# Two attention and expert layers on one core: an addition moved behind the maxima, a copy tied to order, and gathers one step sooner

## The chip, the cores and the metric

The kernel runs on one core of a Trainium2 chip. Its time is that of one launch in microseconds (us) on the device. The core's engines run beside each other, each through its own queue in order: TensorE does matmuls (in the profile PE, and PEld for its weight loads), VectorE (DVE), ScalarE (ACT) and GpSimd (POOL) do the rest, and SyncE (SP) issues most of the transfers (DMAs).

## What is computed

The reference, cut to what matters (4 batches of 512 tokens by 256; a context of 1601 rows per batch; all in float32):

```python
x = x + cross_attention_0(ctx, layernorm(x))   # 8 heads of 128, keys from context and latents, with projections
x = x + experts_0(layernorm(x))                # 8 experts, 2 per token, capacity 512 rows per expert, gelu (tanh)
x = x + cross_attention_1(ctx, layernorm(x))   # 8 heads of 32, queries from x, keys and values from the context
x = x + experts_1(layernorm(x))                # 8 experts, 2 per token, no capacity, gelu (exact), biases
```

In `cross_attention_1` the weights are a softmax over the 1601 context rows:

```python
attn = softmax(q @ k.T * 32 ** -0.5)           # per batch and head: 512 x 1601
out  = attn @ v
```

## The kernel before

The program is one long stream of steps with four stages: the first attention (128 steps of a batch, a head and 128 queries), the first expert layer, the second attention, and the second expert layer. Small work of one stage (routing, layernorms, gathers, projections) is hung by hand into the steps of another, in lists such as `later` and `at`.

**Second attention.** It runs in 16 units. A unit is (batch `b`, half `o` of the channels, half `f` of the queries): four heads of 32 channels, and 256 queries. Units 0 to 3 are batch 0, 4 to 7 batch 1, and so on. A unit has seven steps (`PER_UNIT`), each over 256 context rows; the last has 65. All engines but SyncE follow the program's order here, because the loop stands in `in_order(*computing)`.

One pass of the loop over `step` emits, in this order:

1. `weights(u, s)`: TensorE puts an offset (L1587, four matmuls, one per head) and the scores (L1597) of this step into four banks; ScalarE takes the exponential into the tiles `pT` (L1611; step 0 writes the tiles `sum`).
2. For the step before (`held`): `weigh` (L1633), weights times values, and `add_weights` (L1623).
3. In step 2 of a unit, `closing` of the unit before: transposes and small matmuls (L1671, L1672), then DVE's `inv` and `got` (L1680, L1682), and a closing sum into `x` on GpSimd (L1689).
4. `maxima` (L1329, L1340): TensorE makes a piece of the next unit's scores again in another layout, into four banks, and DVE takes the maxima `tops` out of them, one instruction per head. A unit has six pieces of 512 rows and one short piece of 2 x 65. The short piece falls into step 3.
5. `total` (L1652): matmuls with ones that sum the weights over the context rows.
6. The list `at[step]`: whatever was hung into this step.

`add_weights` adds the tiles `pT` of the steps 1, 3 and 5 onto those of step 0 (`ADDED = (1, 3, 5)`), so that `total` has fewer tiles to sum. Batch 3 adds only step 3 (`ADDED_LATE`). It acts on the `held` step: the tiles of step 1 are added in step 2, those of step 3 in step 4, those of step 5 in step 6. Each time it is two DVE instructions (L1623) of 128 x 1024.

The scores, the offsets and the small tiles beside them share one pool of seven banks:

```python
ps_s = st.enter_context(tc.tile_pool(name="c_ps_s", bufs=7, space=PSUM))
```

A step takes four banks for `weights` and four for `maxima`, and more where small work needs one, so a tile's bank is the one that was taken seven tiles before.

**Gathers for later batches.** `collect(b + 1)` gives eight steps: each fills a tile `g` with zeros (L361) and gathers the rows that the first expert layer made for 128 tokens (L362), both on GpSimd. `add_collected` then multiplies `g` by its share and adds it to `x` (L381, L382, on GpSimd, twice per 128 tokens). After that `queries(b + 1)` takes the layernorm statistics of `x` (L145, L146, L155 on DVE, a root on ScalarE, the rest of L176 to L179 on DVE, L183 on GpSimd) and projects it (L1289). `s0` is the first step of batch `b` (28 per batch); with `b` = 1 and 2, batches 2 and 3 are gathered at `s0 - 14` and the seven steps after it, and their sums follow in two steps.

**Second routing.** `route2(b - 1)` is a generator that is resumed at listed steps; its parts touched here are GpSimd's `extra`, `cnt`, `earlier` and `taken` (L533 to L541), TensorE's two matmuls with them (L547, L550), DVE's `counted` (L554), place arithmetic (L565 to L577), the transposes of its weights (L559) and the addition of a bias product to `x` (L627, which reads a bank of the same pool).

**First routing.** `choose` in `route` picks two experts per token, counts them per expert, and carries the counts of earlier tokens from tile to tile in `taken`: `earlier` (L318) keeps for each of four tiles what was taken before it, and L319 adds the tile's own counts. TensorE uses both (L324, L327). This runs for batches 0 to 2 within the first attention, and for batch 3 within the first expert layer. Outside the second attention the order on an engine is a scheduler's, within what the data allow, unless an instruction is given to `keep_in_program_order`.

Of the kernel before, what the change touches and what calls it, by code (L numbers as in the profile page):

```python
# [13 lines left out]
ALU = mybir.AluOpType  # L14
# [62 lines left out]
def rows_of(i, n, tail):  # L77
    return tail if i == n - 1 else P
# [6 lines left out]
def xattn_ffn_twice(ctx: ExitStack, tc: tile.TileContext, a: dict, out: bass.AP):  # L85
    nc = tc.nc
# [112 lines left out]
    def transposed(psum, tag, dst, src, n):  # L199
        for c in range(DC):  # L200
            turn_part(psum, tag, dst, src, n, c)
# [47 lines left out]
    taken = const.tile([P, E], F32, name="taken")  # L249
# [7 lines left out]
    def route(b, rt, wide_rt, psum, tag):  # L257
# [5 lines left out]
        def small(name):  # L263
            return rt.tile([P, NT], F32, tag=name, name=name)

        def wide(name):
            return rt.tile([P, NT, E], F32, tag=name, name=name)

        def spread(t):
            return t.unsqueeze(2).to_broadcast([P, NT, E])  # L270
# [6 lines left out]
        def choose():  # L277
            xnT = wide_rt.tile([P, DC, S], F32, tag="xnT", name="xnT")
            transposed(psum, tag, xnT, xn, NT)
            ps = psum.tile([P, NT, E], F32, tag=tag, name="ps_l")  # L280
            for t in range(NT):
                for c in range(DC):
                    nc.tensor.matmul(
                        ps[:, t, :],
                        lhsT=xnT[:, c, t * P : (t + 1) * P],
                        rhs=wr[:, c, :],
                        start=c == 0,
                        stop=c == DC - 1,
                    )
            sc, m = wide("sc"), small("m")  # L290
            nc.vector.tensor_copy(sc, ps)
            nc.vector.tensor_reduce(m, sc, AX.X, ALU.max)
            nc.vector.tensor_tensor(sc, sc, spread(m), ALU.subtract)
            nc.scalar.activation(sc, sc, AF.Exp)
            nc.vector.tensor_reduce(m, sc, AX.X, ALU.add)
            nc.vector.reciprocal(m, m)
            nc.vector.tensor_tensor(sc, sc, spread(m), ALU.mult)


            hot, chosen = [], []  # L300
            for k in range(2):
                pk, ck, hk, cand = prob[k][:, mine_b], small(f"c{k}"), wide(f"hot{k}"), wide("cand")
                nc.vector.tensor_reduce(pk, sc, AX.X, ALU.max)
                nc.vector.tensor_tensor(cand, sc, spread(pk), ALU.is_equal)
                nc.vector.scalar_tensor_tensor(cand, cand, -64.0, iota, ALU.mult, ALU.add)
                nc.vector.tensor_reduce(ck, cand, AX.X, ALU.min)
                nc.vector.tensor_tensor(hk, cand, spread(ck), ALU.is_equal)
                nc.vector.tensor_scalar(ck, ck, 64.0, None, ALU.add)
                if k == 0:
                    nc.vector.scalar_tensor_tensor(sc, hk, -4.0, sc, ALU.mult, ALU.add)  # L310
                hot.append(hk)
                chosen.append(ck)


            cnt, earlier = wide("cnt"), wide("earlier")
            nc.vector.tensor_tensor(cnt, hot[0], hot[1], ALU.add)
            for t in range(NT):
                nc.vector.tensor_copy(earlier[:, t, :], taken)  # L318
                nc.vector.tensor_tensor(taken, taken, cnt[:, t, :], ALU.add)  # L319
            if b in (0, B - 2, B - 1):  # L320
                nc.vector.tensor_copy(reached[:, (0, B - 2, B - 1).index(b), :], taken)
            ps = psum.tile([P, NT, E], F32, tag=tag, name="ps_c")
            flat = "p t e -> p (t e)"
            nc.tensor.matmul(  # L324
                ps.rearrange(flat), lhsT=before, rhs=cnt.rearrange(flat), start=True, stop=False
            )
            nc.tensor.matmul(  # L327
                ps.rearrange(flat), lhsT=ones, rhs=earlier.rearrange(flat), start=False, stop=True
            )
            for k in range(2):  # L330
                off, at, mine = small("off"), small("at"), wide("mine")
                nc.vector.tensor_tensor(mine, hot[k], ps, ALU.mult)
                nc.vector.tensor_reduce(off, mine, AX.X, ALU.add)
                nc.vector.scalar_tensor_tensor(at, chosen[k], float(CAP), off, ALU.mult, ALU.add)
                nc.vector.tensor_scalar(off, off, float(CAP), NOWHERE, ALU.is_ge, ALU.mult)
                nc.vector.tensor_tensor(at, at, off, ALU.add)
                nc.vector.tensor_copy(slot[k][:, mine_b], at)
# [305 lines left out]
    def fetched(e, half):  # L643
        n = 1 if half and e in FEW else CT
        sx = b_two.tile([P, CT, D], F32, tag="sx", name="sx")[:, :n]
        nc.sync.dma_start(sx, slots(slot_x, e, half, n))
        w1 = b_two.tile([P, DC, FF], F32, tag="w1", name="w1")
        w2 = b_two.tile([P, FC, D], F32, tag="w2", name="w2")
        nc.sync.dma_start(w1, a["w1"][e].rearrange("(c p) f -> p c f", p=P))
        nc.sync.dma_start(w2, a["w2"][e].rearrange("(c p) d -> p c d", p=P))  # L650
        return e, half, sx, w1, w2
# [34 lines left out]
    with ExitStack() as st:  # L686
# [410 lines left out]
        for n in range(n_steps + 4):  # L1097
            b, h, t = n // (H0 * NT), n // NT % H0, n % NT
# [278 lines left out]
    with ExitStack() as st:  # L1377
# [75 lines left out]
        first = fetched(0, 1)  # L1453
# [103 lines left out]
    with ExitStack() as st:  # L1557
# [18 lines left out]
        def keys_of(s):  # L1576
            return range(2 * s, min(2 * s + 2, NM))
# [39 lines left out]
        def added(u):  # L1617
            return ADDED if units[u][0] < B - 1 else ADDED_LATE

        def add_weights(u, s, pTs):  # L1620
            if s in added(u):
                for to, pT in zip(sums[u], pTs):
                    nc.vector.tensor_tensor(to, to, pT, ALU.add)  # L1623

        def weigh(u, s, pTs, ps):

# [15 lines left out]
        def total(u, s, pTs, ps):  # L1642

            of = [(s, pTs)] if s and s not in added(u) else []
            if s == PER_UNIT - 1:
                of.append((0, sums.pop(u)))
            for s0, tiles in of:
                js = keys_of(s0)
                r = rows_of(js[-1], NM, TAIL)
                for k in range(len(js)):  # L1650
                    for i in range(HG):
                        nc.tensor.matmul(  # L1652
                            ps[i * DH1 : (i + 1) * DH1, QH:],
                            lhsT=ones[:r, :DH1],
                            rhs=tiles[i // 2][:r, i % 2, k * QH : (k + 1) * QH],
                            start=False,
                            stop=s0 == 0 and k == 1,
                            skip_group_check=True,
                        )
# [120 lines left out]
        for b in range(B):  # L1780
            s0 = per_batch * b
            if b:
                place(s0, route2(b - 1, one, side, "s", far=far), routed if b + 1 < B else last_routed)
            if b + 1 < B:
                got, steps = collect(b + 1)
                first = s0 if b == 0 else s0 - 14
                for k, f in enumerate(steps):
                    put(first + (k // 2 if b == 0 else k), f)
                for t in range(NT):
                    put(  # L1790
                        (first + 4 if b == 0 else first + 7) + t // 2,
                        lambda b=b, got=got, t=t: add_collected(b + 1, got, (t,), nc.gpsimd),
                    )
                place(s0, queries(b + 1, qTs), asked[b + 1])
# [19 lines left out]
        held, ending = None, {}  # L1814
        for step in range(PER_UNIT * n_units + 5):
            u, s = divmod(step, PER_UNIT)
            fresh = (u, s, weights(u, s)) if u < n_units else None
            if held:
                if held[1] == 0:
                    ps_of = ps_o.tile([P, 2 * QH], F32, tag="o", name="ps_o1")  # L1820
                weigh(*held, ps_of)
                add_weights(*held)
            next(ending.pop(step, iter(())), None)
            for g in ahead.pop(step, ()):
                maxima(*g)
            if held:
                total(*held, ps_of)
                if held[1] == PER_UNIT - 1:
                    ending[step + 2] = closing(held[0], ps_of)
                    next(ending[step + 2])  # L1830
            for f in at.pop(step, []):
                f()
            held = fresh
# [6 lines left out]
    with ExitStack() as st:  # L1840
# [252 lines left out]
        more = [lambda e=e: first_tile(e) for e in range(2, E)]  # L2093
# [12 lines left out]
        for i in range(n):  # L2106
            w, xT, to, share = here
# [153 lines left out]
```

## Time and profile before

| what | value |
|---|---|
| time, median of 3 runs (lowest, highest) | 2684.9 us (2683.66, 2690.97) |
| the profiled execution | 2684.01 us |
| its span, first to last instruction | 2682.0 us |
| mean granted TensorE clock | 0.997 |
| busy share of TensorE, DVE, ACT, POOL | 98%, 49%, 33%, 14% |
| second attention, about 1861.9 to 2385 us | TensorE busy 507.6 of 523.1 us, DVE 377.2, ACT 261.2, POOL 193.5 |
| two additions L1623, start of the first to start of what follows | 2.27 us |
| one maximum L1340, 128 x 512 and 128 x 130 | 0.69 and 0.29 us, 0.6 and 0.2 us apart |
| one pair L381 and L382 on GpSimd | 1.72 us |

The profile is of one execution. Its timeline gives for each instruction the start from the beginning of the span, its length, the engine, the line, what it writes and reads, and in brackets how long the engine sat idle before it and what ended that. The view of waits sums such idle time by who waited for whom. A busy TensorE is not TensorE at its peak, because matmuls are pipelined and their ends are modelled.

### The profile page before, as it was taken

The numbers are of one execution on the slowest core, as the hardware profiler recorded it, in microseconds if no ns is written. First come the engines' busy times: TensorE is split into PE (matmuls) and PEld (weight loads), VectorE is DVE, ScalarE is ACT, GpSimd is POOL, SyncE is SP. The second block draws the span as 40 slices with busy tenths as digits, with TensorE's granted clock in tenths as the row PEclk, the third lists the DMA queues.
The fourth block names the chain that finished last, engine by engine and source line by source line (L and its number), as shares of the span: only waits on it lengthen the run. The fifth ranks groups of instructions, "written<-read, shape, count | busy, mean of one in ns | idle before, by whom it ended". The sixth has DMA issues, their size and how long they took to land. (4 is left out here: it accounts for less than half of the span.)

```text
span 2682.0 us, 38424 instructions
## 1 busy us (share of the span) xinstructions
PE 2625.5 (98%) x14748; PEld 1785.6 (67%) x14748; DVE 1319.7 (49%) x2307; ACT 898.2 (33%) x1589; POOL 372.2 (14%) x485
## 2 busy tenths in 40 slices
PE   7999999999999999999999999999999999999997
PEld 3666676666666666667667678877454454468887
DVE  6544547644456544454544442134777777642111
ACT  4333233323333322333233322122554445452221
POOL 0000000100000100000100000101442531334442
PEclk9999999999999999999999999999999999999999
DMA  6444434433443433433443464643443100036663
GB/s 181 120 114 113 101 93 114 104 93 89 107 115 87 115 94 87 98 91 86 108 99 89 124 200 142 209 158 101 126 126 120 64 32 5 23 113 187 193 219 78
DMA packets 191324, 302.91 MB, mean 113 GB/s; under 512 B 41783, under 2 KB 113272, under 8 KB 188440
## 3 DMA queue, kind: packets, MB, share of 16 engines
q1 hardware_dynamic: 152392, 218.33, 29.4%
q0 software_dynamic: 14160, 46.31, 5.9%
q10 hardware_dynamic: 24576, 35.68, 5.2%
q8 instruction: 119, 1.95, 0.3%
q14 instruction: 77, 0.63, 0.1%
HBM read 111.46 MB, written 51.07 MB: 61 GB/s over the span
## 5 line engine op out<-in xcount | busy, mean ns | idle before, releaser
L995 DVE TENSOR_REDUCE top<-ps_s 128x1 f32<-128x2113 f32 x128 | 301.7, 2357 | 592.1 <-PE ps_s L987 587.1
L1024 PE MATMUL ps_o<-pT,v 128*128 128x256 f32 x2176 | 519.1, 380 | 0.4 <-DVE inv L1002 0.4
L987 PE MATMUL ps_s<-kT,qT 128*128 128x512 f32 (+1 forms) x1280 | 486.6, 524 | 2.6 <-ACT attn L1001 2.6
L1024 PEld LDWEIGHTS ps_o<-pT,v 128*128 128x128 f32 x2176 | 407.9, 190 | 112.6 <-issue 66.8
L1001 ACT ACTIVATE attn<-ps_s,top 128x2113 f32<-128x2113 f32 x128 | 258.9, 2023 | 492.7 <-DVE top L995 461.6
L987 PEld LDWEIGHTS ps_s<-kT,qT 128*128 128x128 f32 x1280 | 241.1, 190 | 249.3 <-issue 237.9
L1016 DVE STREAM_TRANSPOSE pT<-swapped 128x2176 f32<-128x2176 f32 x128 | 312.4, 2441 | 34.0 <-DMA swapped<-attn 25.8
L1340 DVE TENSOR_REDUCE tops<-ps_s 128x1 f32<-128x512 f32 (+2 forms) x428 | 251.6, 649 | 140.8 <-PE ps_s L1329 140.7
L933 PE MATMUL ps_k<-kvin,wkv 128*128 128x512 f32 (+2 forms) x640 | 259.3, 528 | 2.8 <-DVE kvin L823 2.4
L970 PE MATMUL ps_v<-wkv,kvin 128*128 128x256 f32 x1088 | 254.5, 381 | 2.1 <-ACT v L977 2.1
L970 PEld LDWEIGHTS ps_v<-wkv,kvin 128*128 128x128 f32 x1088 | 204.5, 190 | 36.1 <-ACT v L977 6.2
L1611 ACT ACTIVATE pT<-ps_w 128x512 f32<-128x512 f32 (+1 forms) x384 | 184.3, 565 | 119.4 <-PE ps_w L1597 118.6
L949 ACT ACTIVATE kT<-ps_k,bqk 128x512 f32<-128x512 f32 (+1 forms) x192 | 101.0, 555 | 268.9 <-PE ps_k L933 126.0
L933 PEld LDWEIGHTS ps_k<-kvin,wkv 128*128 128x128 f32 x640 | 116.0, 192 | 75.4 <-issue 64.4
L977 ACT COPY v<-ps_v 128x512 f32<-128x512 f32 x144 | 80.0, 561 | 215.5 <-PE ps_v L970 131.0
L1329 PE MATMUL ps_s<-kv,qT 32*128 32x512 f32 (+1 forms) x1024 | 123.8, 550 | 0.0
L1597 PE MATMUL ps_w<-qT,kv 32*128 32x256 f32 (+1 forms) x1664 | 118.3, 382 | 0.0
L757 POOL TENSOR_TENSOR x<-x,bo 128x256 f32<-128x256 f32 x16 | 11.8, 768 | 724.1 <-DVE lat L183 532.1
L670 PE MATMUL ps_h<-sxT,w 128*128 128x256 f32 (+1 forms) x512 | 108.0, 367 | 0.6 <-DVE x L1045 0.6
L1393 PE MATMUL ps_y<-w,hT 128*128 128x256 f32 x480 | 107.8, 380 | 0.0
L670 PEld LDWEIGHTS ps_h<-sxT,w 128*128 128x128 f32 x512 | 91.9, 190 | 17.7 <-issue 4.2
L1393 PEld LDWEIGHTS ps_y<-w,hT 128*128 128x128 f32 x480 | 90.3, 190 | 14.9 <-issue 2.4
(328 smaller groups left out, 2736.2 us busy)
## 6 DMA issues: line engine op xcount, KB each, us to landing
swapped<-attn SPq DMA_DIRECT2D x1536, 68.0 KB
swapped<-attn ACTq DMA_DIRECT2D x512, 68.0 KB
w<-in_w_dram SPq DMA_DIRECT2D x32, 1024.0 KB
rows_b<-empty SPq DMA_DIRECT2D x36, 530.0 KB
w_e<-in_wall_dram SPq DMA_DIRECT2D x5, 2052.0 KB
cw<-in_ctxT_dram SPq DMA_DIRECT2D x4, 1601.0 KB
ctx_b<-in_ctx_dram SPq DMA_DIRECT2D x3, 1536.0 KB
slot_x<-scrap SPq DMA_DIRECT2D x8, 512.0 KB
```

The lines of the kernel that those rows point to most:

```text
L670: nc.tensor.matmul(ps[:, f, :], lhsT=w1[:, c, (f0 + f) * P : (f0 + f + 1) * P], rhs=sxT[:, c, :], start=c == 0, stop=c == DC - 1,)
L933: nc.tensor.matmul(ps[:, :n], lhsT=wkv[:, c, hs], rhs=kvin[:, c, : n // 32, k, :] if k < 4 else flat_kvin[c][:, left : left + P], start=c ...
L970: nc.tensor.matmul(ps[:, k, :], lhsT=flat_kvin[c][:, j * P : (j + 1) * P], rhs=wkv[:, c, cols], start=c == 0, stop=c == DC - 1,)
L987: nc.tensor.matmul(flat[:, j0 : j0 + n], lhsT=qT[:, t * P : (t + 1) * P], rhs=kT[:, j0 : j0 + n], start=True, stop=True,)
L995: nc.vector.tensor_reduce(top, flat[:, :L], AX.X, ALU.max, negate=True)
L1001: nc.scalar.activation(attn[:, :L], flat[:, :L], AF.Exp, bias=top, accum_out=total)
L1016: nc.vector.transpose(pT[:, :, k * P : (k + 1) * P].rearrange("p c (a i) -> p a c i", a=4), swapped.rearrange("p a (c i) -> p a c i", i=32),)
L1024: nc.tensor.matmul(ps, lhsT=v[:, j - parts[part][0], (h % 2) * DH0 : (h % 2 + 1) * DH0], rhs=pT[:, j, :], start=j == 0, stop=j == NB - 1,)
L1329: nc.tensor.matmul(pss[i][:, at : at + n], lhsT=qTs[b][rows, o, q0 : q0 + P], rhs=kvs[b][0][o][rows, j0 : j0 + n], start=True, stop=True,)
L1340: nc.vector.tensor_reduce(tops[u][:, t : t + at // n, some, j0 // 512], of, AX.X, ALU.max,)
L1393: nc.tensor.matmul(ps[:, t, :], lhsT=hT[:, f, t * P : (t + 1) * P], rhs=w2[:, f, :], start=f == 0, stop=f == FC - 1,)
L1611: nc.scalar.activation(pT[:r, i, :n], pss[2 * h + i][:r, :n], AF.Exp)
```

## The change

Four places are edited. In `choose`, the copy L318 of the first tile is kept in program order (for every batch). In `add_weights` a parameter `behind` is new; the loop calls it for step 1's tiles behind `maxima` and not before them. The gathers of batches 2 and 3, and with them their sums, are hung one step sooner (`s0 - 15`). `asked`, the steps at which the queries' layernorm is taken, is unchanged.

```diff
             for t in range(NT):
-                nc.vector.tensor_copy(earlier[:, t, :], taken)
+                carried = nc.vector.tensor_copy(earlier[:, t, :], taken)
+                if t == 0:
+                    tc.keep_in_program_order(carried)
                 nc.vector.tensor_tensor(taken, taken, cnt[:, t, :], ALU.add)
...
-        def add_weights(u, s, pTs):
+        def add_weights(u, s, pTs, behind=False):
             if s in added(u):
                 for to, pT in zip(sums[u], pTs):
-                    nc.vector.tensor_tensor(to, to, pT, ALU.add)
+                    more = nc.vector.tensor_tensor(to, to, pT, ALU.add)
+                    if behind:
+                        tc.keep_in_program_order(more)
...
                 got, steps = collect(b + 1)
-                first = s0 if b == 0 else s0 - 14
+                first = s0 if b == 0 else s0 - 15
                 for k, f in enumerate(steps):
                     put(first + (k // 2 if b == 0 else k), f)
...
                 weigh(*held, ps_of)
-                add_weights(*held)
+                if held[1] != 1:
+                    add_weights(*held)
             next(ending.pop(step, iter(())), None)
             for g in ahead.pop(step, ()):
                 maxima(*g)
             if held:
+                if held[1] == 1:
+                    add_weights(*held, behind=True)
                 total(*held, ps_of)
```

## The prediction

> **What bounds the kernel now.** First the page's busy line: TensorE (PE) is the bound, and the rest is idle time of 56 us, so a change of order can only act through what PE waits for.
>
> ```profile
> PE 2625.5 (98%) x14748; PEld 1785.6 (67%) x14748; DVE 1319.7 (49%) x2307; ACT 898.2 (33%) x1589; POOL 372.2 (14%) x485
> ```
>
> Then the waits of PE, who waited for whom (us in total, times, longest). The first line lies in the second attention (1861.9 to about 2385 us), the second at one place of the first attention.
>
> ```profile
> PE ps_w L1587 <- DVE tops L1340: 13.7, 30, 1.4
> ...
> PE ps_v L970 <- ACT v L977: 2.1, 1, 2.1
> ```
>
> Then the timeline of one step that the change touches: unit 6, steps 2 and 3 (I write 6.2, 6.3; a step begins where PE starts the four L1587). VectorE (DVE) first, then PE; columns are start, length, instruction, count, and in brackets the idle time before it with its releaser.
>
> ```profile
> 2074.47 2.35 DVE L1623 TENSOR_TENSOR sum<-sum,pT 128x1024 f32<-128x1024 f32 x2
> ...
> 2077.92 2.48 DVE L1340 TENSOR_REDUCE tops<-ps_s 128x1 f32<-128x512 f32 x4 [0.31 <-PE ps_s L1329]
> ...
> 2080.97 0.19 DVE L513 TENSOR_TENSOR wb<-wb,totw 128x32 f32<-128x32 f32 x1
> 2081.52 0.89 DVE L1340 TENSOR_REDUCE tops<-ps_s 128x2 f32<-128x130 f32 x4 [0.36 <-PE ps_s L1329]
> 2082.33 2.35 DVE L1623 TENSOR_TENSOR sum<-sum,pT 128x1024 f32<-128x1024 f32 x2
> ```
>
> ```profile
> 2077.72 0.39 PE L1587 MATMUL ps_w<-below,ones_b 6*128 6x512 bf16 x3
> 2078.66 0.37 PE L1587 MATMUL ps_w<-below,ones_b 6*128 6x512 bf16 x1 [0.55 <-DVE tops L1340]
> ...
> 2082.43 0.40 PE L1587 MATMUL ps_w<-below,ones_b 6*128 6x512 bf16 x4
> ```
>
> Seven banks rotate. With four for the weights and four for the maxima in a step, the fourth weights bank of a step is the one that the first maximum of the step before reads. So PE stops at 2078.66, when the first of the maxima that began at 2077.92 has ended. That costs 0.94 us (the fourth start less the first). But those maxima did not wait for the addition, done at 2076.82: the bracket names PE's own scores. The same 0.55 us gap with PE as the releaser stands in units 1, 2, 3, 4, 6 and 10.
>
> **The addition (12 units, batches 0 to 2).** Nothing is added or removed: two L1623 per unit move behind the four maxima of step 2. As built, the orders of PE, ScalarE and SP are the same before and after; only DVE's and POOL's differ. Two additions hold DVE's queue for 2.27 us (at 2093.36 and 2094.49, next start 2095.63). What was their cover, DVE waiting for PE's closing transposes, is left empty; behind them now stand the small work of step 2, the short maxima of step 3 (0.2 us apart) and the bank that step 4's fourth L1587 needs. In unit 6: DVE free at 2081.16, later by 2.27 = 2083.43 (scores ready 2081.52, so the queue decides); first short maximum and handing over 0.34, 2083.77; PE wants the bank at 2082.43. Stall 1.34. That such lateness stops PE the trace shows already, where layernorm statistics make 7.3's short maxima late (PE, PE, DVE):
>
> ```profile
> 2116.56 0.39 PE L1587 MATMUL ps_w<-below,ones_b 6*128 6x512 bf16 x3
> 2117.17 0.37 PE L1587 MATMUL ps_w<-below,ones_b 6*128 6x512 bf16 x1 [0.21 <-DVE tops L1340]
> ```
>
> ```profile
> 2116.85 0.86 DVE L1340 TENSOR_REDUCE tops<-ps_s 128x2 f32<-128x130 f32 x4
> ```
>
> The same sum for the others, as DVE free before / step 4 begins / stall: unit 1 1910.53 / 1911.48 / 1.66; 2 1942.90 / 1944.93 / 0.58; 3 1976.64 / 1977.58 / 1.67; 5 2044.53 / 2047.00 / 0.14; 9 2188.06 / 2190.54 / 0.13; 10 2224.38 / 2225.66 / 1.33; 11 2256.65 / 2258.16 / 1.10, less 0.08 because its step-2 maxima did start late. Unit 4 has 1.98 us of query projection between: none. Unit 0 is the one case that the edit is good for: maxima at 1873.43 could start at 1872.9, a gain of 0.53, and lose 0.60 in step 4. Unit 3 pays 0.25 more, since its root's input (L155) comes late to ScalarE ahead of step 5's exponentials. Unit 8: behind the additions stands L627 (2151.79 to 2152.47), which reads a bank that PE takes next for a quarter of step 3's scores (one more tile is in the rotation here); it would end 2.27 later, at 2154.74, and PE wants the bank at 2152.90: 1.9, rounded up. The later addition (step 3's) ends before step 4's scores in each unit, since PE is late too. Without unit 7: 1.66+0.58+1.67+0.25+0.14+1.34+1.9+0.13+1.33+1.02+0.07 = 10.1.
>
> The trace does not show the additions beside GpSimd (POOL) at the new places; beside its arithmetic two of them took 2.73 instead of 2.35 (2107.72), so each stalled unit lies between 0 and 0.4 more. I take 0: POOL is mostly idle there.
>
> [...]
>
> **Gathers and sums one step sooner.** POOL runs in order, so I look at what the sums overtake. The eight gathers themselves (1.0 each to issue, on POOL's own queue; their buffers are long free) only move into POOL's idle time. For batch 2 (units 1 to 3) they and the sums overtake a closing sum that nobody awaits: nothing. DVE's two additions there no longer meet POOL's arithmetic, which I count as nothing too. For batch 3 the built order puts the sums of two row tiles, four pairs L381 and L382, ahead of the carried counts L538 to L541. POOL, then PE:
>
> ```profile
> 2099.80 1.04 POOL L362 DMA_INDIRECT g<-slot_y,slot  x1 [0.27 <-POOL g L361]
> 2100.88 0.25 POOL L538 TENSOR_TENSOR cnt<-hot,hot 128x32 f32<-128x32 f32 x1
> ...
> 2102.68 0.19 POOL L540 COPY earlier<-taken 128x8 f32<-128x8 f32 x1
> ...
> 2106.51 0.92 POOL L381 TENSOR_SCALAR g<-g,prob 128x256 f32<-128x256 f32 x1
> 2107.51 0.72 POOL L382 TENSOR_TENSOR x<-x,g 128x256 f32<-128x256 f32 x1
> 2108.22 2.94 POOL L381 TENSOR_SCALAR g<-g,prob 128x256 f32<-128x256 f32 x1
> ```
>
> ```profile
> 2107.11 0.39 PE L550 MATMUL ps_c<-earlier,ones 128*128 128x32 f32 x2
> ```
>
> A pair takes 1.72 (2106.51 to 2108.22, rounded up), four 6.9. The last copy ends at 2102.87, so at 2109.77; L550 wants it at 2107.11. The slack of 4.2 is used up and PE waits 2.7, with the whole of step 7.2 queued behind it. In return:
>
> ```profile
> 2120.56 0.43 DVE L145 BATCH_NORM_STATS2 st<-x 128x6 f32<-128x256 f32 x1 [2.30 <-POOL x L382]
> ```
>
> DVE waits here for the last sum, and PE pays: steps 7.4 and 7.5 lose 0.61 and 2.36 on L1587 (2122.34 to 2124.70), and 0.87 on 7.5's scores (2.01 instead of 1.14), held by exponentials behind a late root; 3.84 in all. After: DVE free at 2113.84 + 2.27 additions + 1.21 place work (unit 11's row) + 1.07 statistics = 2118.39, first maximum 2118.73, PE at 2116.56: 2.17; step 7.5 has no bank stall, but the root is still late, 0.85. So 3.02 for 3.84, a gain of 0.8; unit 7 nets 2.7 - 0.8 = +1.9.
>
> On L381's 2.94: it lies beside the two additions, its equals take 0.92. [...]
>
> **Counts tied to order.** Four copies of 0.17 come 0.2 us into their own chain; PE's L327 follows it, 0 to 0.2 each; I take 0, four matmuls of L1035 lie beside it. One evacuation (L124) goes ahead of a 0.17 us copy (L321): nothing. But the copy for the last batch leaves this place (DVE, PE):
>
> ```profile
> 1315.56 0.17 DVE L318 COPY earlier<-taken 128x8 f32<-128x8 f32 x1 [7.52 <-DMA slot_x<-xn,slot]
> 1315.66 2.36 DVE L995 TENSOR_REDUCE top<-ps_s 128x1 f32<-128x2113 f32 x1
> ```
>
> ```profile
> 1323.58 0.70 PE L970 MATMUL ps_v<-wkv,kvin 128*128 128x256 f32 x2 [2.07 <-ACT v L977]
> ```
>
> It held DVE for a scatter whose buffer it takes over; the maximum behind it started 2.8 late (scores done 1312.83), the exponential and ACT's v copies after it too, and PE lost 2.07. All of it comes back: 2.07, bounded by 0 and 2.8.
>
> **Sum.** 10.1 + 1.9 - 2.1 = +9.9, all on PE, so it moves the end. The profiled execution took 2684.01 (span 2682.0 and 2.0 around it; the median shown is 2684.9): 2693.9.
>
> **Rivals.**
> (a) The additions do hold the banks, and their new place is covered. Then the step-3 stalls go (units 1, 2, 3, 4, 6, 10, 7 and 11 at 0.9, unit 0 at 1.5: 8.7), with unit 7's 3.2 in step 5 and the 2.1: 2670.0. For it: the waits' first line names DVE. Against: the brackets name PE. It decides if step 2's maxima start before PE's scores let them, which they cannot. 6%.
> (b) The new place costs nothing, because the short maxima's bank isn't the next one wanted. Left are +2.7 - 3.8 - 2.1: 2680.8. Against: 7.4. 14%.
> (c) As forecast, but PE does not stand at POOL's counts: 2691.2. Against: the order is fixed on both queues. 18%.
> The forecast has 62%.
>
> **Range and chances.** Low: (c) less the stall of unit 8 and with the 2.8 is 2688.6, and half of (b) is to be taken in: 2685. High: 0.4 for nine units, 0.8 for copies, and 2.1 that stays away, 6.5 together, not all at once: 2699. A run can tell about 0.3%, or 8 us from the median: 2676.8 to 2693.0. Faster is (a) and some of (b): 7%. Same is the rest of (b), most of (c) and the low edge of the forecast: 29%. Slower 64%.
>
> **What would show it.** Right: L1587 waits on maxima in step 4 of units 1, 3, 6 and 10, about 1 us each, with the step-3 gaps of 0.55 still there; a wait of PE's ps_c on POOL of 2 to 3 us near 2110; unit 8's ps_s waiting for L627; no 7.5 us wait at L318, no 2.1 us at L970. Wrong: step 3 shortened from 4.7 to 3.8 us in units 1 to 4, or step 4 beginning no later than now.

## The result, and the profile after

Before 2684.69 us (median of 6, 2683.66 to 2690.97), after 2698.86 (6 runs, 2695.83 to 2700.24): ratio 1.0046, 95% interval 1.0036 to 1.0056. The interval lies wholly above 1: the change makes the kernel slower by about half a per cent, and it ends 5.0 us later than forecast. The profiled execution of after took 2698.88, its span is 2696.8, 14.8 longer than before's. A second set (below, e10) gave 2694.88 beside 2684.05.

PE is as busy as before, 98%, but its busy time grew by 11.9 us with the same 14748 matmuls. A wait would add idle time; this is the first sign that something made matmuls longer.

```profile
PE 2637.4 (98%) x14748; PEld 1790.7 (66%) x14748; DVE 1318.4 (49%) x2307; ACT 898.0 (33%) x1589; POOL 370.5 (14%) x485
```

The waits of PE (total, times, longest). Lines after the edits stand 2 higher, later ones up to 4: L1587 is L1589, L1340 L1342, L627 L629, L538 L540, L547 and L550 are L549 and L552, L1623 L1625. Of the lines of 0.9 us and more three are new, at the three places named in the forecast; the 2.1 us of ScalarE's v copies at the old L970 are gone.

```profile
PE ps_w L1589 <- DVE tops L1342: 15.1, 30, 1.2
...
PE ps_s L1331 <- DVE x L629: 1.5, 1, 1.5
PE ps_c L552 <- POOL earlier L542: 1.3, 1, 1.3
...
PE ps_c L549 <- POOL cnt L540: 0.9, 1, 0.9
```

The timeline of unit 6, steps 2 to 4, DVE and then PE. The additions stand behind the maxima and ahead of the small work and the short maxima. The 0.55 in front of step 3's fourth bank is still there, for PE's own scores still release the maxima (0.31 in the bracket). New is the 0.86 in front of step 4's: the step is 1.23 us longer than before, and 1.34 were forecast for this stall.

```profile
2082.14 2.48 DVE L1342 TENSOR_REDUCE tops<-ps_s 128x1 f32<-128x512 f32 x4 [0.31 <-PE ps_s L1331]
2084.54 2.35 DVE L1625 TENSOR_TENSOR sum<-sum,pT 128x1024 f32<-128x1024 f32 x2
...
2087.46 0.19 DVE L515 TENSOR_TENSOR wb<-wb,totw 128x32 f32<-128x32 f32 x1
2087.57 0.89 DVE L1342 TENSOR_REDUCE tops<-ps_s 128x2 f32<-128x130 f32 x4
```

```profile
2081.95 0.39 PE L1589 MATMUL ps_w<-below,ones_b 6*128 6x512 bf16 x3
2082.88 0.37 PE L1589 MATMUL ps_w<-below,ones_b 6*128 6x512 bf16 x1 [0.55 <-DVE tops L1342]
...
2086.66 0.39 PE L1589 MATMUL ps_w<-below,ones_b 6*128 6x512 bf16 x3
2087.91 0.37 PE L1589 MATMUL ps_w<-below,ones_b 6*128 6x512 bf16 x1 [0.86 <-DVE tops L1342]
```

Unit 7, step 1: GpSimd's last early sum ends at 2113.24, and only then come the counts; PE stands twice.

```profile
2112.52 0.72 POOL L384 TENSOR_TENSOR x<-x,g 128x256 f32<-128x256 f32 x1
2113.20 0.25 POOL L540 TENSOR_TENSOR cnt<-hot,hot 128x32 f32<-128x32 f32 x1
...
2115.00 0.19 POOL L542 COPY earlier<-taken 128x8 f32<-128x8 f32 x1
```

```profile
2110.59 2.00 PE L1232 MATMUL ps_v<-cw 128*128 128x256 f32 x8
2113.50 0.41 PE L549 MATMUL ps_c<-cnt,before 128*128 128x32 f32 x2 [0.92 <-POOL cnt L540]
2115.24 0.64 PE L552 MATMUL ps_c<-earlier,ones 128*128 128x32 f32 x2 [1.33 <-POOL earlier L542]
2115.81 0.61 PE L1589 MATMUL ps_w<-below,ones_b 6*128 6x512 bf16 x4
2116.21 1.92 PE L1599 MATMUL ps_w<-qT,kv 32*128 32x256 f32 x16
```

The last line carries what the forecast had not: the sixteen entries of the scores take 1.92 where they take 1.03 elsewhere, and no bracket stands there. The view of windows tells why (columns: stretch, its length, busy time of PE, PEld, DVE, ACT and POOL with the count, then the granted clock, the DMA share and GB/s). First after, at this place; then before, at about the same.

```profile
2114.90:2128.50 13.60, 13.26 (x92) 6.73 (x92) 6.04 (x12) 4.43 (x9) 7.61 (x12) 0.50 0.15 41
```

```profile
2111.00:2124.00 13.00, 11.28 (x130) 5.85 (x127) 10.08 (x27) 5.29 (x10) 9.71 (x13) 1.00 0.23 62
```

TensorE's clock was halved for 13.65 us, four times 3.41. The clock records of after show three more such stretches in the second attention, of 3.41 us each (from 1927.2, 2067.1 and 2166.1); before's show none there.

Where the 14.8 us of span went, by the lengths of the steps, after less before:

| part | forecast | after |
|---|---|---|
| copy, at its place | -2.07 | -2.24 |
| stalls behind the additions, all units but 7 | +10.1 | +8.9 |
| PE at GpSimd's counts (7.1) | +2.7 | +2.9 |
| steps 7.4 and 7.5 | -0.8 | -2.9 |
| halved clock: 2.0, 6.0, 7.2, 7.3, 8.3 | not in the sum | +10.1 |
| rest (start of the span, other steps, last stage) | 0 | -2.0 |

In step 8.3 the stall and the halved clock lie in one step, 3.56 longer. The stall's share is taken from e10, where the same step is 1.97 longer at full clock. The rest is mostly before's own profile: a second one of it (e11) has a last stage 2.0 shorter.

### The profile page after: what moved, and what is told of

It reads as the page before. It is cut to its first block, busy times and chain, and to the rows that moved or that the text cites. A ratio compares the mean times of both kernels' runs of the same rounds, so it can differ in the third digit from the quotient of the medians.

```text
span 2696.8 us, 38430 instructions
## 1 busy us (share of the span) xinstructions
PE 2637.4 (98%) x14748; PEld 1790.7 (66%) x14748; DVE 1318.4 (49%) x2307; ACT 898.0 (33%) x1589; POOL 370.5 (14%) x485
## 3 DMA queue, kind: packets, MB, share of 16 engines
q8 instruction: 119, 1.95, 0.3%
## 5 line engine op out<-in xcount | busy, mean ns | idle before, releaser
L1342 DVE TENSOR_REDUCE tops<-ps_s 128x1 f32<-128x512 f32 (+2 forms) x428 | 251.3, 649 | 133.3 <-PE ps_s L1331 133.2
L1599 PEld LDWEIGHTS ps_w<-qT,kv 32*128 32x128 f32 (+1 forms) x1664 | 83.6, 182 | 32.0 <-issue 28.2
```

What stands on the lines that cost most here:

```text
L1342: nc.vector.tensor_reduce(tops[u][:, t : t + at // n, some, j0 // 512], of, AX.X, ALU.max,)
L1599: nc.tensor.matmul(pss[i][:r, k * QH : (k + 1) * QH], lhsT=kvs[b][0][o][rows, j * P : j * P + r], rhs=qTs[b][rows, o, f * QH : (f + 1) * Q ...
```

## The experiments

Theory: the additions hold banks by DVE's queue; the counts stand behind sums on GpSimd; the copy held DVE; and on top the clock is halved behind some of PE's waits. Rivals: the additions' new place is free and something else costs; the halved clock comes at random, or with any wait, or only with one long idle stretch. Ratios are to the kernel before on the same chip.

**e1, the addition alone** (`add_weights` and its two calls as in the change, nothing else).

> The kernel before with one part of the change alone: step 1's two additions behind the maxima. Theory (the additions stand in front of the short maxima of step 3, whose bank step 4 wants): L1587 stalls in step 4 of units 1, 3, 6, 10, 11 of 1.0 to 1.6 us and about 0.5 in units 0 and 2, 1.5 on unit 8's scores behind L627; 8 us of stalls, less 0.5 to 1 in unit 7; the wait of the L145 on GpSimd's sum goes, since DVE is late itself. 2692 us at a full clock, up to 2697 if the clock is halved after some of the stalls. Rival (GpSimd's order does the harm, the addition is nearly free): below 2688.

2691.88 (2690.64 to 2692.63), ratio 1.0035 [1.0023, 1.0048]. Most of the loss is the addition's. The step-4 stalls are those of after within 0.01 in units 1, 3, 6 and 10 (1.56, 1.55, 1.23, 1.23), and three windows of 3.41 us are at half clock: 6.83 us behind a stall of 2.7 in 7.4, and one behind unit 8's 1.5.

**e2, the copy alone**

```diff
-                nc.vector.tensor_copy(earlier[:, t, :], taken)
+                carried = nc.vector.tensor_copy(earlier[:, t, :], taken)
+                if t == 0:
+                    tc.keep_in_program_order(carried)
```

> The kernel before with the copy of the carried counts tied to order alone. Theory: DVE's wait of 7.5 us at 1315 us and TensorE's of 2.1 us behind it go, the second attention begins 2.5 us sooner as it did in the changed kernel: 2682 us. Rival (the copy in its chain delays TensorE's product of the counts in each batch and gives it back): 2684 to 2686.

2680.21 (2678.57 to 2684.67), ratio 0.9995 [0.9985, 1.0005]: too little to tell by time. The trace says more. Compared at the same matmuls, PE gains 2.24 us between 1318 and 1322 in after and 2.23 or 2.24 in every kernel here with the copy tied; without it 0.34 and 0.45 in e3 and e1, and nothing in before's second profile.

**e3, the gathers and sums alone**

```diff
-                first = s0 if b == 0 else s0 - 14
+                first = s0 if b == 0 else s0 - 15
```

> The kernel before with batches 2 and 3 gathered and summed one step sooner, alone. Theory: TensorE waits 2.3 to 2.7 us for GpSimd's counts in unit 7, the 3.8 us of steps 7.4 and 7.5 come back: 2683.5 at a full clock; if the clock is halved behind the wait, as it was in the changed kernel for 13.65 us, 5 us more: 2689. Rival (the halved clock there came from the additions): 2683 to 2684.5, with the granted clock at 1.0 through unit 7.

2684.41 (2680.61 to 2686.93), ratio 1.0006 [0.9997, 1.0016]. Step 7.1 is 2.70 longer, 7.4 and 7.5 are 2.70 shorter: without the additions the sums' sooner end gives back what the counts cost. The clock stayed full behind the two waits at the counts (0.91 and 1.33), as the rival had it. But e9, which moves no addition either, has the same waits and a halved window behind them, so the additions are not what decides.

**e4, the copy, and the queries' statistics of batch 3 one step later** instead of sooner sums

```diff
-            3: (-5, -4, -3, -2, 0, 1, 3, 9, 9),
+            3: (-4, -3, -2, -1, 0, 1, 3, 9, 9),
```

> The kernel before with the copy tied, and in place of the sooner gathers the layernorm statistics of batch 3 one step later (its first four steps at -4 to -1 from the batch, before at -5 to -2). Theory: DVE no longer stands for GpSimd's last sum in step 7.4, GpSimd's order stays, so the 3.2 us of step 7.5 and the 2.5 us of the copy are both gained: 2679 us. Rival (the statistics one step later meet the exponentials or the place work and stall TensorE again): 2681 to 2683.

2682.01 (2677.76 to 2683.18), ratio 0.9996 [0.9987, 1.0006]. The 3.78 of 7.4 and 7.5 came back in full. But GpSimd's `xn` was late, PE stood two times 0.9 at L196, its clock was halved for one window behind them, and 7.6 to 8.1 lost 4.75. A stall was moved, not removed.

**e6, half a dose**: of the two additions one stays ahead of the maxima.

```diff
-                if held[1] != 1:
-                    add_weights(*held)
+                add_weights(*held, some=slice(0, 1) if held[1] == 1 else slice(None))
...
-                    add_weights(*held, behind=True)
+                    add_weights(*held, behind=True, some=slice(1, 2))
```

> The changed kernel, but of the two additions of step 1's tiles only one is moved behind the maxima; the other stays ahead of them. Theory (the additions make DVE late, and PE stops only by what the lateness exceeds the slack in front of step 4's bank; on top come stretches of halved clock that appear where short PE waits lie close together): the lateness is 1.13 us less than in the changed kernel, so the waits of L1589 in step 4 shrink to about 0.4 in units 1 and 3, 0.1 in units 6 and 10, nothing in units 0, 2 and 11, and unit 8's wait for the bias product from 1.5 to about 0.4: 1.4 in all for 8. Unit 7 as in the changed kernel (PE waits about 2.25 for GpSimd's counts, 2.9 come back). With 2.5 for the copy that is 1 to 2 us below the kernel before, and fewer stretches of halved clock than the changed kernel's seven windows of 3.4 us, 1.6 us for each that stays: 2681 to 2689. Rival (each addition costs its share wherever it stands, so half of the addition's 8.9 us): 2685 or more, with step-4 waits of half the size in every unit. Rival (the halved clock has nothing to do with the waits): still some seven halved windows, 2691.

2685.83 (2681.74 to 2688.34), ratio 1.0006 [0.9997, 1.0015]. Step 4 of units 1 and 3 lost 0.42 each, where two additions cost 1.55: one addition less is 1.13 less, as the sum has it. Units 2, 6, 10 and 11 lost nothing. Unit 8's wait fell to 0.32, and its clock stayed full:

```profile
2156.78 0.66 PE L1331 MATMUL ps_s<-kv,qT 32*128 32x65 f32 x12 [0.32 <-DVE x L629]
```

A cost in proportion would have shown half: 0.8 in units 1 and 3, and 0.6 in units 6 and 10. So the slack decides. The 13.65 us of half clock behind the counts are the same as in after.

**e7, the wait at the counts filled**: ten matmuls ahead of the counts' first, into their own bank; the results are overwritten.

```diff
+        if b == 0:
+            bank = psum.tile([P, 4, P], F32, tag=tag, name="ps_c2")
+            for i in range(FILL):
+                nc.tensor.matmul(bank[:, i % 4, :], lhsT=ones, rhs=ident, start=True, stop=True)
```

> The changed kernel with ten matmuls of 128x128 into the bank of the counts, ahead of the first of the two count matmuls of batch 0's second routing, so that TensorE works while it would wait for GpSimd's counts in unit 7; their results are overwritten and the computation is unchanged. Theory (the clock is halved because of the waits): the waits of about 0.9 and 1.3 us on GpSimd nearly go, step 7.1 is as long as in the changed kernel (the counts come when they come), and the long stretch of halved clock in steps 7.2 and 7.3 (13.65 us, 5.3 us of time) goes or shrinks to at most 3.4: about 2693 where the changed kernel has 2698, with a mean clock of 0.995 instead of 0.993. Rival (the stretch does not come from these waits): it stays, 2698, the clock 0.993. Rival (the fillers cost time themselves since the counts are not what ends last): step 7.1 longer by up to 1.7, 2700.

2697.31 (2695.55 to 2698.25), ratio 1.0048 [1.0035, 1.0061]: not the 2693 expected. PE's timeline (ten fillers are twenty entries at L551, the counts L558 and L561; lines are 9 higher than after's):

```profile
2110.89 2.39 PE L551 MATMUL ps_c<-ident,ones 128*128 128x128 f32 x20
...
2113.74 0.41 PE L561 MATMUL ps_c<-earlier,ones 128*128 128x32 f32 x2 [0.31 <-POOL earlier L543]
2114.08 0.39 PE L1598 MATMUL ps_w<-below,ones_b 6*128 6x512 bf16 x4
2114.31 1.03 PE L1608 MATMUL ps_w<-qT,kv 32*128 32x256 f32 x16
...
2125.99 0.58 PE L1598 MATMUL ps_w<-below,ones_b 6*128 6x512 bf16 x1 [2.38 <-DVE tops L1351]
2125.99 2.28 PE L1608 MATMUL ps_w<-qT,kv 32*128 32x256 f32 x16
```

The stretch behind the counts is gone: scores 1.03 again, 7.2 and 7.3 as long as before (5.27 less than in after). But PE, on time now, meets the late maxima of 7.4: 2.38, the stall that the forecast had put at 2.17 and that after, slowed, did not show. Behind it the clock is halved for a window. So the half clock of after had covered that stall, and filling one wait moved the loss 12 us on.

**e8, the gathers sooner, the sums where they were**, with the copy tied and no addition moved. The counts stay ahead of the sums on GpSimd.

```diff
-                first = s0 if b == 0 else s0 - 14
+                first = s0 if b == 0 else s0 - 15
...
-                        (first + 4 if b == 0 else first + 7) + t // 2,
+                        (first + 4 if b == 0 else first + 8) + t // 2,
```

> The kernel before with the copy tied and the gathers of batches 2 and 3 one step sooner, but their sums in their old steps, so that the carried counts stay ahead of the sums on GpSimd. No addition is moved. Theory: TensorE does not wait at the counts in unit 7 (step 7.1 as long as before), and the sums still end a little sooner because no gather stands between them, so of the 2.9 us that the sooner sums save in steps 7.4 and 7.5 some 1 to 2 are kept; with the copy's 2.5, and up to one stretch of halved clock more or less (1.6): 2678 to 2681 where the kernel before has 2683. Rival (the sums' old steps decide, the gathers are no part of it): steps 7.4 and 7.5 as before, 2680.5 to 2682, as with the copy alone.

2679.46 (2676.81 to 2682.95), ratio 0.9985 [0.9976, 0.9994]: the one version whose whole interval lies below 1. The copy's 2.23 is in it. Step 7.1 is unchanged, and 7.5 is 1.71 shorter: its bank stall fell from 1.38 (idle time at 2124.10 before) and 0.23 to this:

```profile
2119.80 0.37 PE L1589 MATMUL ps_w<-below,ones_b 6*128 6x512 bf16 x1 [0.23 <-DVE tops L1342]
```

The sums, in their old steps, still end sooner: DVE's L145 waits 0.58 for the last of them where it waited 2.30.

**e9, the change without its addition** (copy, gathers and sums).

> The change without its addition: the copy tied, gathers and sums one step sooner. Theory: the change's loss is the addition's. Step 7.1 longer by 2.7 to 2.9, steps 7.4 and 7.5 shorter by 2.7 to 2.9, the copy 2.5 sooner, no waits in step 4, and at most two windows of halved clock: 2680 to 2683 where the kernel before has 2683. Rival (the long halved stretch comes from the wait at the counts alone): steps 7.2 and 7.3 at half clock here too, 5 us more: 2686 to 2688. Rival (the parts help or hurt each other): anything more than 2 us off the sum of the copy alone (-2.5) and the gathers alone (+1.4 by the medians).

2683.63 (2679.89 to 2688.72), ratio 1.0001 [0.9992, 1.0009], and steps 7.1, 7.4 and 7.5 by +2.68, -0.58, -2.42. One window is at half clock in 7.2, one in 12.0.

**e10 and e11, the changed kernel and the one before again**, for a second profile of each.

> The changed kernel once more, for a second profile and a time on the same chip as the next. Theory (the stretches of halved clock come from TensorE's waits, and a window's place on its own grid decides where one wait is enough): the stretch in steps 7.2 and 7.3, behind the two waits for GpSimd's counts, and the one behind unit 8's wait for the bias product (1.46 us) are there again; the single windows in units 2 and 6, where the kernel before has the same waits without them, may be gone or elsewhere. Time 2695 to 2700, ratio 1.004 to 1.006, mean clock 0.992 to 0.995. Rival (the windows fall at random): at 7.2 and 8.3 the clock is full this time.

> The kernel before once more, for a second profile. Theory: full clock in steps 7.2, 7.3 and 8.3, no wait at the counts, at most one or two single windows of 3.4 us elsewhere in the second attention; 2680 to 2687. Rival (random windows): as many as in the changed kernel, five to seven.

After 2694.88 (2693.14 to 2695.80), ratio 1.004 [1.0027, 1.0054]; before 2683.43 in one run. The step-4 stalls of the second profile of after equal those of the first within 0.01, but three windows of the second attention are at half clock, not seven: one behind the counts, one behind a 1.67 in 7.4, one in 10.1; none in 2.0, 6.0 or 8.3. Before again has none in the second attention. So "always behind these waits" does not hold, and the counts' window in both profiles of after, with none in either of before, speaks against "random".

Laid side by side, all beginnings and ends of the stretches within one execution fall on one grid of 3.413 us (in after the stretches that begin at 1927.15 and 2067.10 lie 41 such windows apart; the last stretch of each ends off it, with the program). So I summed PE's idle time window by window of each profile's grid. Two profiles of after itself differ at unit 8's wait of 1.46, the same in both. First the first profile, with the window that holds the wait and the one behind it, then the same in e10:

```profile
2162.67:2166.08 3.41, 1.95 (x36) 1.19 (x32) 2.88 (x4) 2.06 (x4) 1.43 (x2) 1.00 0.13 47
2166.08:2169.49 3.41, 3.41 (x22) 1.49 (x21) 3.16 (x6) 0.00 (x0) 0.97 (x1) 0.50 0.68 233
```

```profile
2160.60:2164.01 3.41, 2.09 (x29) 1.24 (x30) 2.85 (x7) 0.55 (x2) 1.95 (x2) 1.00 0.37 126
2164.01:2167.42 3.41, 3.41 (x40) 1.60 (x38) 1.57 (x2) 1.30 (x3) 0.97 (x1) 1.00 0.35 112
```

In the first the whole wait lies in one window, busy 1.95: the next has clock 0.50. In e10 the grid cuts it, busy 2.09: full clock. These two windows, idle for 1.46 and 1.32, gave my estimate that about 1.4 us of idle time within one window decides at these waits, and two more kernels test it.

**e12 and e13, five fillers and one**: e9 with e7's lines, and `FILL` of 5 and of 1.

> The change without its addition, with five matmuls of 128x128 into the counts' own bank ahead of the first count matmul of batch 0's second routing; their results are overwritten. Theory (the clock is halved for the next 3.41 us when TensorE was idle for more than about 1.4 us of one window of a fixed 3.41 us grid, no matter in how many pieces): the two waits of 0.9 and 1.33 us become one of about 1.0, below the threshold, so the clock in steps 7.2 and 7.3 is full; step 7.1 as long as without the fillers (the counts come when they come). Rival (any wait at this place halves the clock): half the clock in 7.2 again. Time 2679 to 2684.

> The same with one such matmul. Theory: about 2.0 us of idle time remain, so the clock is halved in the step behind it if at least 1.4 us of them lie in one window of the grid; where the grid cuts them, it stays full, and the windows' idle time says which. Rival (a matmul in the gap is enough, since then no single idle stretch counts): full clock wherever the grid lies. Time 2680 to 2686.

2679.53 and 2679.07, one run each. PE's waits at the counts, then windows; e12 first, e13 second:

```profile
2107.16 0.38 PE L558 MATMUL ps_c<-cnt,before 128*128 128x32 f32 x2
2108.87 0.41 PE L561 MATMUL ps_c<-earlier,ones 128*128 128x32 f32 x2 [1.33 <-POOL earlier L543]
```

```profile
2107.39:2110.80 3.41, 2.08 (x32) 1.42 (x35) 1.49 (x3) 0.31 (x1) 2.89 (x9) 1.00 0.12 39
2110.80:2114.21 3.41, 3.41 (x37) 1.54 (x26) 3.04 (x5) 2.20 (x5) 3.33 (x4) 1.00 0.14 43
```

```profile
2104.74 0.41 PE L558 MATMUL ps_c<-cnt,before 128*128 128x32 f32 x2 [0.69 <-POOL cnt L541]
2106.48 0.41 PE L561 MATMUL ps_c<-earlier,ones 128*128 128x32 f32 x2 [1.33 <-POOL earlier L543]
```

```profile
2104.54:2107.95 3.41, 1.88 (x24) 1.39 (x24) 1.02 (x2) 0.00 (x0) 2.81 (x11) 1.00 0.15 52
2107.95:2111.37 3.42, 3.42 (x30) 2.06 (x30) 2.18 (x3) 2.06 (x4) 3.34 (x3) 0.50 0.14 43
```

Step 7.1 is 2.70 longer in both. With five fillers 1.33 of the window are idle (I had expected 1.0; only the first wait was filled) and the clock stays full; with one, 1.54 in two pieces (0.20 and 1.33), and it is halved for two windows. Both rivals fall at this place, each by one profile: a wait is not enough, and one long idle stretch is not needed. The other kernels with these waits fit. The window that holds most of them has 1.34 idle in e3, and the clock stays full; it has 1.88 in e6, 1.89 in after, 2.14 in e10 and 2.19 in e9, and the clock is halved in each.

## Why the prediction was right or wrong

The sign held, and so did the mechanism in each place that it named. What the sum left out is, in the first profile of after, the largest single term of the result.

1. **Step 3's gaps stay, rival (a).** They do (0.55 in 6.3, with PE in the maxima's bracket), and in unit 0, named as the one exception, step 3 gained 0.61 and step 4 lost 0.48 (0.53 and 0.60 forecast).
2. **Stalls in step 4.** Forecast and measured in after: unit 1 1.66 and 1.55, 2 0.58 and 0.48, 3 1.67 and 1.56, 6 1.34 and 1.23, 10 1.33 and 1.23, 11 1.02 and 0.99. The nearly constant excess of 0.1 is not in the handing over, which came out at its 0.34 (in 6.4 from the short maximum at 2087.57 to the bank at 2087.91). It lies in "DVE free", which the forecast took as the end of the small work: by the trace DVE starts what stands next some 0.08 before such an end (L515 ends at 2087.65, the short maximum starts at 2087.57). Units 5 and 9 were within that 0.1 of none, and nothing shows there; nor does unit 3's late root (0.25). Unit 8: PE idles 1.46, and the step is 1.97 longer at full clock (e10), for 1.9. Together 8.9 for 10.1. The bound of 0.4 more beside GpSimd wasn't needed: two additions took 2.35 as before. Rival (b) is out by the step-4 rows.
3. **Counts.** At full clock 2.68 to 2.73 (e3, e7, e9, e10, e12, e13) for 2.7; the end of after's 2.93 lies in the halved clock. PE stands twice, at L549 too, which needs the first count; the forecast had named L550 alone. Rival (c) is out. The early pairs took 0.92 to 0.94 and 0.72 to 0.73 each, no 2.94 among them.
4. **What comes back in 7.4 and 7.5.** The 0.8 was right for a PE on time: e7 has +3.76 and -2.87, and the halved window in it costs about 1.7 (half of 3.41), so -0.8. In after the half clock made PE late and the stall fell away, hence -2.9 beside +5.3.
5. **Copy.** -2.24 for -2.07, within its bounds; four copies in their chain cost no more than 0.1 each time. In e11 a window of half clock follows PE's wait at L970, which by my estimate (half of 3.41) costs that execution another 1.7 at this place.
6. **The step that failed** is the sum's premise that time is what PE waits for: it gave the clock no term, without a reason. Beside the waits, and mostly behind them, stand windows of half clock: 10.1 us in the profile of after, of which about 2.1 only replace the stall of point 4. In after's other runs the time goes with the mean clock, from 2695.83 at 0.995 to 2700.24 at 0.992.
7. **Luck.** 2698.86 lies 0.1 us inside the upper end of the stated range, but that end was made of 0.4 for nine units, 0.8 for copies and 2.1 that stays away, and none of the three came. In e10 2694.88 is near 2693.9. There, by the step lengths, about 4 us of half clock stand beside stalls 1.2 smaller than the sum's and a rest of -2.0, so the nearness is in part luck too.

Why the two sets differ by 4 us stays open. The place of the waits in the grid, which differs between the two profiles, may decide it; but all five runs of e10 are shorter than all six of the first set, so something that stays the same within a set, such as the chip, is not ruled out.

## What to carry to other kernels

An instruction moved into an engine's idle time is free only if what stands behind it in the queue has slack to the next wanted bank: subtract, place by place, as e6 shows (1.13 less lateness, 1.13 less stall, and none where slack was left). When TensorE bounds a kernel, look at the granted clock beside the waits: in this kernel's second attention, waits that added up to 1.46 us or more in one window of the grid were followed by half clock, and in after a single window of half clock made its step longer by 1.63 (2.0), 1.64 (6.0) and 1.59 us (8.3, its 3.56 less the 1.97 of e10). To make later work sooner, moving its transfers alone and leaving its arithmetic behind whatever another engine waits for was the better of the two here (e8: 7.1 unchanged and 7.5 shorter by 1.71; e9: 7.1 longer by 2.68, 7.4 and 7.5 shorter by 3.00).

## What the runs showed of the hardware that was not expected

Across the 14 profiles of this case, every window of the second attention that ran at full clock and in which PE was idle for 1.46 us or more of 3.41, 12 of them, was followed by half clock (among them 1.46 and 1.89 in after, 1.54 in e13, 1.88 in e6, 2.14 in e10 and 2.19 in e9). Of those with 1.0 to 1.4, three were and some fifty were not (1.38 was in e4, and was not in before). So this is a strong tendency there, and not yet a rule.

The same profiles show that it doesn't carry over to the first attention. At the old L970 three windows had more than 1.46 us of idle time. One was followed by half clock (e11), two were not: e3, below, and e1 with 1.62. First e11, then e3:

```profile
1319.39:1322.81 3.42, 1.36 (x7) 0.86 (x5) 0.16 (x2) 0.74 (x2) 0.00 (x0) 1.00 0.59 149
1322.81:1326.22 3.41, 3.41 (x9) 2.70 (x9) 0.00 (x0) 0.61 (x2) 0.00 (x0) 0.50 0.51 120
```

```profile
1320.32:1323.73 3.41, 1.68 (x8) 1.15 (x8) 0.00 (x0) 1.35 (x3) 0.00 (x0) 1.00 0.76 191
1323.73:1327.15 3.42, 3.42 (x14) 2.26 (x13) 0.00 (x0) 0.96 (x2) 0.00 (x0) 1.00 0.49 115
```

Nor is idle time the only thing that half clock follows. Seven more stretches of the second attention began after windows with 0.63 us of it or less (0.58 and 0.63 in after, ahead of the stretches in 2.0 and 6.0), five of them with none: each of those five holds sixteen entries of the router's matmuls (L481 before; for each a weight of 128x128 in 0.19 us and a product of 128x8). But fifteen other windows that hold all sixteen entries were followed by full clock, in before the one from 2066.33 for example. So these entries alone do not decide it, and what does is not shown. How long the clock stays halved behind a wait is open too: four windows in after and e6, two in e1 and e13, one in e9 and e10.
